# End of attention: the order of VectorE's and ScalarE's side work around the last norms, and the residual in the context's buffer

## The chip, the cores and the metric

One core of one Trainium2 chip runs the whole program. The time is device microseconds of one execution, from launch to end; of several executions the median is given. A profile is one execution recorded by the hardware profiler; its span runs from the first to the last instruction of the program. Five engines work side by side, each through its own instructions strictly in the order in which they stand in the built program: TensorE (PE; its weight loads are PEld), VectorE (DVE), ScalarE (ACT), GpSimd (POOL) and SyncE (SP), which here only issues transfers (DMA).

## The reference

A pre-norm block in float32 on 2048 rows of 1024: attention across the 32 heads of one position (each position's heads attend to each other, not to other positions), then a gated feed-forward whose weights are first rounded to the 16 NF4 levels in blocks of 64.

```python
q = (h @ wq.T + bq).reshape(B, S, H, D)       # k, v alike; h = layernorm(x)
scores = einsum('bshd,bstd->bsht', q, k) / sqrt(D)
context = einsum('bsht,bstd->bshd', softmax(scores), v)
x = x + context.reshape(B, S, E)
# feed-forward on layernorm(x); dq = round to NF4 times the block's largest absolute value
h = silu(y @ dq(w1).T) * (y @ dq(w2).T)       # y = layernorm(x)
x = x + h @ dq(w3).T
```

## The kernel before

**Tiles and stages.** The 2048 rows are 16 tiles of 128 rows, numbered 0 to 15, and 8 pairs `p`. Three sweeps run over the pairs: the projection to q, then to k with scores and softmax, then to v with the context product. The feed-forward follows, on blocks of 512 columns of a transposed, normalised x. The large products use seven products on quarter matrices in place of eight (`products` in attention, `Unit` in the feed-forward), so sums and differences of quarters are formed beforehand (`A`, `V`, the tiles `xU`) and the partial results are put together by copies on ScalarE and additions on VectorE.

**The side work.** While TensorE runs attention and the feed-forward, VectorE and ScalarE round the feed-forward's weights. The generator `background` does this in small steps: a step is one `sg` on ScalarE (L266, 128x1024) and one select-and-merge on VectorE that reads it (L267); there are also steps without ScalarE (L257, L259, L261), a block maximum with a reciprocal (L230, L237, L238), and scalings by the block's value (L218, 16 instructions of ScalarE, or L214, one of VectorE). The `sg` tile has two buffers, so the third step's ScalarE part waits for the first step's VectorE part. `advance(n)` puts the next n steps into the program. `flush` puts in the transposes of a finished weight (L178 on TensorE, copied by L179, combined by L185 to L194, stored by L197).

**What sets the order.** TensorE's instructions stand in the order in which the program writes them. On the other engines a scheduler orders them when the kernel is built, by when it thinks them ready. Two helpers bind it. `behind(kind)` sets a step's ScalarE part (kind "step") or scaling (kind "scale") behind the last copy that was passed to `marked`, if the kind is in `urgent["rule"]`. `turn()`, used by `advance`, sets the VectorE part of the steps behind the instruction in `held["behind"]`, if there is one.

**The end of the v sweep.** `gather(i, ...)` makes one tile's attention output, in two parts: the first half of the context product (L464, into PSUM), and then the second half with `residual`. That one transposes the result on VectorE out of PSUM into `cx` (L725, a single buffer), adds the row's x in place into `x1` (L729), sends the sum to `x1d` in memory in two halves (L731), and calls `normed(x1, x1)`: statistics (L133), their combination (L134), the inverse deviation on GpSimd (L137, L138), and the normalised tile written over x1 (L358). The context product has one PSUM tile of four banks, so the next tile's first half waits for this tile's L725. `part()` emits the next part in line, `keep_T(i)` transposes tile i's normalised x on TensorE (L768), copies it to `xT` (L769, marked), stores it (L774), and for each odd tile forms four differences `xU` on VectorE (L784, two buffers) and stores them (L785).

In the last pass of the v sweep (p = 7) the second half of tile 11, both halves of tile 12 and the first half of tile 13 are emitted. The five parts left, the second half of tile 13 and both halves of tiles 14 and 15, are put between the eight groups of matmuls of `plain_block`, which is the feed-forward's chunk 0 on the first 512 columns (L364 with `z<-xB,w0`; its gates are L895 and L896). Behind each part stands an `advance`. Then the first feed-forward unit starts: `first` makes z and copies it to g0 (L975), `middle` goes on accumulating into the same z bank, so each further product into z (L364 `z<-xT`) waits for the copy before it: g0 (L975), u2 (L982), u4 (L989).

SyncE's queue carries, in one order, the loads of x, weights and operands and the stores L731, L774, L785 and L197.

Of the kernel before, what the change touches and what calls it, by code (L numbers as in the profile page):

```python
# [14 lines left out]
ALU = mybir.AluOpType  # L15
# [16 lines left out]
TB = 512  # L32
# [37 lines left out]
def preln_block_kernel(  # L70
# [14 lines left out]
    nc = tc.nc  # L85
# [13 lines left out]
    x1d = [  # L99
        [tc.dram_tile([P, TB], FP, name=f"x1d{i}_{n}") for n in range(2)] for i in range(NT)  # L100
    ]
# [9 lines left out]
    hook = {"scale": "ACT"}  # L111

    urgent = {"last": None, "rule": ()}

    def marked(ins):

        urgent["last"] = ins.ins
# [6 lines left out]
    held = {"behind": None}  # L124

    def turn():

        return tc.issue_after(held["behind"]) if held["behind"] else nullcontext()

    def mean_var(pool, src, dst):  # L130
        st = pool.tile([P, 2, 6], FP, tag="st", name="st")
        for j in range(2):
            nc.vector.bn_stats(st[:, j, :], src[:, ts(j, 512)])  # L133
        nc.vector.bn_aggr(dst, st.rearrange("p a b -> p (a b)"))  # L134

    def inv_std(dst, var):
        nc.gpsimd.tensor_tensor(dst, var, eps, ALU.add)  # L137
        return nc.gpsimd.tensor_tensor(dst, dst, mhalf, ALU.pow)  # L138
# [141 lines left out]
    def advance(n):  # L280
        for _ in range(n):
            with turn():
                next(bg, None)

    def until(kind, c):
        while (kind, c) not in wd:
            if pending:
                flush(1)
            else:
                advance(1)  # L290
# [15 lines left out]
    NP = NT // 2  # L306
# [43 lines left out]
    def normed(src, dst, order=None):  # L350
        mv = small.tile([P, 2], FP, tag="mv", name="mv")
        rs = small.tile([P, 1], FP, tag="rs", name="rs")
        mean_var(small, src, mv)
        with tc.issue_after(order["last"]) if order else nullcontext():
            order_end = inv_std(rs, mv[:, 1:2])
        if order is not None:
            order["last"] = order_end.ins
        done = nc.vector.tensor_scalar(dst, src, mv[:, 0:1], rs, ALU.subtract, ALU.mult)  # L358
        hook["normed"] = done.ins
        return dst  # L360

    def mm4(dst, w, xop, start, stop):
        for k in range(4):
# [7 lines left out]
            )  # L371

    def products(A, fill, used=lambda name: None, apart=None):


# [216 lines left out]
    def load_A(src, p):  # L592
        t = pair.tile([P, 7, 4, P], FP, tag="A", name="A", bufs=2)
        nc.sync.dma_start(t, src[p])
        return t
# [81 lines left out]
    def part():  # L677
        if parts:
            next(parts[0])
            left_over[0] -= 1  # L680
            if left_over[0] == 0:
                parts.pop(0)
                left_over[0] = 2
# [38 lines left out]
    def residual(i, at, x1):  # L722

        cx = work.tile([P, E], FP, tag="cx", name="cx")
        nc.vector.transpose(  # L725
            cx.rearrange("p (h d) -> p d h", d=D),
            at[:, :, 0:256].rearrange("p c (s d) -> p d s c", d=D),
        )
        nc.vector.tensor_tensor(x1, x1, cx, ALU.add)  # L729
        for n in range(2):  # L730
            nc.sync.dma_start(x1d[i][n], x1[:, ts(n, TB)])  # L731
        return normed(x1, x1)

    ops = {}

# [51 lines left out]
    for p in range(NP):  # L787
        if p + 1 < NP:
            nextA = load_A(opV, p + 1)
        else:  # L790

            until("2", 0)
            nextA = work.tile([P, 4, 4, P], FP, tag="w0", name="w0")
            nc.sync.dma_start(nextA, wd["2", 0][:, 0:4])
        i = 2 * p - 4

        def fill(n):
            if n in (7, 2, 5, 4) and (p, n) != (1, 7):
                part()
            advance({7: 2, 6: 2, 5: 1, 3: 2}.get(n, 0))  # L800
            if n in (7, 4):
                flush(1)
            if n == 5 and i in x1n:
                keep_T(i, x1n.pop(i))
            if n == 3:
                if p == 0:
                    part()
                elif i + 1 in x1n:
                    keep_T(i + 1, x1n.pop(i + 1))

        cs = products(A, fill, (lambda name: None) if p + 1 < NP else next_op)
        flush(1)
        if p == 0:
            sweep.close()
            sweep = ExitStack()
            work = sweep.enter_context(
                tc.tile_pool(name="workv", bufs=1, side="right", reuse_waits="tile")
            )
        pl = load_tiles(pD, p, "pl", 3)
        for j in range(2):  # L820
            t = work.tile([P, 32, D], FP, tag="vd", name="vd", bufs=3)
            v_T(t, cs[j], vb_sb)
            parts.append(gather(2 * p + j, pl[j], t))
        advance(2)
        A = nextA
    hook["scale"] = "both"
    urgent["rule"] = ()
    left.close()


# [50 lines left out]
    def plain_block(w, tbp):  # L881

        hs = []
        for j in range(2):
            zs = []
            for m in range(2):
                z = ps_z.tile([P, TB], FP, tag="z", name="z")
                mm4(z, w[:, 2 * m], op(f"B1{j + 1}", tbp), True, False)
                yield
                mm4(z, w[:, 2 * m + 1], op(f"B2{j + 1}", tbp), False, True)  # L890
                zs.append(z)
                if not (j and m):
                    yield
            h = h0p.tile([P, TB], FP, tag=f"h{j}", name="h")
            nc.scalar.activation(h, zs[0], AF.Silu)  # L895
            nc.vector.tensor_tensor(h, h, zs[1], ALU.mult)  # L896
            hs.append(h)
        yield hs
# [6 lines left out]

    plain = plain_block(A, 0)
    i = NT - 4
    next(plain)  # L910
    next(plain)
    part()
    advance(1)
    next(plain)
    keep_T(i, x1n.pop(i))
    part()
    advance(2)
    flush()
    next(plain)
    part()  # L920
    advance(2)
    next(plain)
    keep_T(i + 1, x1n.pop(i + 1))
    part()
    advance(3)
    next(plain)
    part()
    advance(3)
    next(plain)
    keep_T(i + 2, x1n.pop(i + 2))  # L930
    hs = {0: next(plain)}
    advance(3)
    held["behind"] = hook["normed"]
    keep_T(i + 3, x1n.pop(i + 3))
    sweep.close()
    sweep_at.close()
# [20 lines left out]
    class Unit:  # L957
# [13 lines left out]
        def first(self):  # L971
            self.z = ps_z.tile([P, TB], FP, tag="z", name="z")
            self.mul(1, self.z, True, False)
            self.g0 = hp.tile([P, TB], FP, tag="g0", name="g0", bufs=2)
            nc.scalar.copy(self.g0, self.z)  # L975

        def middle(self):
            q = self.q = ps_q.tile([P, TB], FP, tag="q", name="q")
            self.mul(7, q, True, False)
            self.mul(6, self.z, False, False)  # L980
            u2 = self.u2 = hp.tile([P, TB], FP, tag="u2", name="u2")
            nc.scalar.copy(u2, self.z)  # L982
            r = ps_r.tile([P, TB], FP, tag="r", name="rr")
            self.mul(2, r, True, True)
            nc.vector.tensor_tensor(self.g0, self.g0, r, ALU.add)  # L985
            nc.scalar.activation(self.g0, self.g0, AF.Silu)
            self.mul(5, self.z, False, False)
            u4 = hp.tile([P, TB], FP, tag="u4", name="u4")
            nc.scalar.copy(u4, self.z)  # L989
            self.h = [new_h(), new_h()]  # L990
            nc.vector.tensor_tensor(self.h[1], u4, q, ALU.add)

# [195 lines left out]
    for n, (g, tbp) in enumerate(passes):  # L1188
        half, sides = None, []
        while now is not None and now.tbp == tbp and now.c in g:  # L1190
            unit = now
            unit.middle()
            if unit.c == min(g[-1], NFULL - 1):
                for c in [c for c in w3T if c not in g]:
                    del w3T[c]
                ask_w3(g)
            if g[-1] == NFULL and unit.c == NFULL - 1:
                half = Half(tbp)
                half.part(0)
                hs[unit.c] = unit.last()  # L1200
                half.part(1)
                hs[NFULL] = half.h
                now = None
            if units:
                now = Unit(*units.pop(0))
                now.first()
            if unit.c < PAIRED and unit.c % 2:
                side = Sides(hs[unit.c - 1], n == 0, len(sides))
                hs[unit.c] = unit.last(side.second)
                sides.append(side.both(hs[unit.c][0]))  # L1210
            elif half is None:
                hs[unit.c] = unit.last()
        if sides:
            down7(g, tbp, sides)
        else:
            down(g, tbp, hs)
        hs = {}
# [40 lines left out]
```

## Time and profile before

| | us |
|---|---|
| median of 4 runs | 2464.74 (2462.41 to 2465.62) |
| the profiled execution, its own time | 2467.89 |
| its span | 2466.1 |

Mean granted TensorE clock 0.991 of full speed.

| stretch, us | stage | PE busy | DVE busy | ACT busy |
|---|---|---|---|---|
| 535 to 745 | v sweep | 204.80 | 194.75 | 100.08 |
| 745 to 770 | its last pass | 22.92 | 20.54 | 13.96 |
| 770 to 835 | plain block, last norms, start of the first unit | 47.81 | 56.71 | 32.47 |
| 905 to 1000 | feed-forward, first group | 91.68 | 88.00 | 75.11 |
| 2200 to 2345 | feed-forward, side work done | 145.00 | 19.13 | 30.27 |
| 2345 to 2466 | last group | 112.52 | 30.20 | 7.16 |

The profile counts a matmul of float32 as two passes, so a group of four 128x512 matmuls is shown as eight. In the lines of a timeline the columns are: start, duration, engine, line of the code, operation, written and read tiles, shapes, count of merged instructions, and in brackets the idle time of the engine ahead of it and what ended it. Names of tiles are shortened to the variable's stem: `x` is x1, `r` the weight being rounded, `g` g0.

### The profile page before, as it was taken

What the parts mean: (1) busy time and instruction counts of PE and PEld (TensorE: products, weight loads), DVE (VectorE), ACT (ScalarE), POOL (GpSimd) and SP (SyncE); (2) the same over time, 40 slices, a digit from 0 to 9 for tenths busy, and PEclk for the clock granted to TensorE, in tenths of its full rate; (3) what the DMA queues carried; (4) which work ended last, traced back from release to release, by engine and by line L of the source; (5) the groups of instructions that cost most, each with busy time, mean ns of one, the idle gap of its engine ahead of it and who ended that gap; (6) DMA issues with size and microseconds to landing.
All of it is one profiled execution on the core that took longest, in us unless ns stands there. A gap on an engine that the chain in (4) does not pass through costs nothing.

```text
span 2466.1 us, 36345 instructions
## 1 busy us (share of the span) xinstructions
PE 2384.6 (97%) x14000; PEld 1115.5 (45%) x14000; DVE 2016.2 (82%) x2239; ACT 1511.9 (61%) x2819; POOL 289.3 (12%) x364
## 2 busy tenths in 40 slices
PE   8899999999998899999999999999999999999998
PEld 4444455545554344444444444444444444444433
DVE  8999888679899799898989989899898998861022
ACT  4556644134445578778787786977878778751200
POOL 1010000000000003030030301203012030020300
PEclk9999999999999999999999999999999999999999
DMA  8788643656779578485784858848588385772983
GB/s 320 274 299 340 244 154 123 227 210 218 237 236 320 192 268 171 141 172 186 280 185 141 175 167 297 176 149 181 161 295 193 126 187 162 276 168 76 179 307 123
DMA packets 179549, 513.87 MB, mean 208 GB/s; under 512 B 15984, under 2 KB 70256, under 8 KB 156976
## 3 DMA queue, kind: packets, MB, share of 16 engines
q1 hardware_dynamic: 138672, 438.08, 49.2%
q0 software_dynamic: 40704, 73.47, 18.4%
q8 instruction: 110, 1.80, 0.3%
q14 instruction: 63, 0.52, 0.1%
HBM read 283.69 MB, written 227.80 MB: 207 GB/s over the span
## 4 chain that ended last, share of the span: by engine, by line
DVE 27%; issue 18%; PE 11%; ACT 8%; DMA 4%; POOL 1%; DVEq 0%; POOLq 0%; ACTq 0%; SPq 0%
DVE r L267 18%; PE z L364 4%; DMA x1d<-acc 2%; ACT sg L266 2%; ACT wn L218 2%; PE q L364 2%; ACT r L218 1%; PE z L1070 1%; DVE r L259 1%; DVE r L261 1%; PE po L1151 1%; DVE am L230 1%; ACT acc L1083 1%; PE rr L364 1%; DMA xdT<-xU 1%
## 5 line engine op out<-in xcount | busy, mean ns | idle before, releaser
L267 DVE SCALAR_TENSOR_TENSOR r<-sg,r 128x1024 f32<-128x1024 f32 x780 | 945.8, 1213 | 81.6 <-ACT sg L266 48.1
L266 ACT ACTIVATE sg<-wn 128x1024 f32<-128x1024 f32 x780 | 814.2, 1053 | 306.5 <-DVE r L267 280.8
L1085 POOL DMA_DIRECT2D x1d<-acc x280 | 243.6, 921 | 1279.0 <-ACT acc L1083 1243.1
L364 PE MATMUL z<-xB,w 128*128 128x512 f32 x720 | 325.6, 599 | 5.9 <-ACT u L989 4.3
L364 PE MATMUL z<-xT,w 128*128 128x512 f32 x656 | 298.5, 598 | 12.1 <-ACT g L975 8.0
L364 PE MATMUL q<-xT,w 128*128 128x512 f32 x656 | 291.3, 592 | 0.0
L1070 PE MATMUL z<-w,h 128*128 128x512 f32 x496 | 230.7, 593 | 2.5 <-ACT acc L1083 2.5
L364 PEld LDWEIGHTS z<-xB,w 128*128 128x128 f32 x720 | 134.3, 191 | 169.4 <-issue 151.2
L364 PEld LDWEIGHTS z<-xT,w 128*128 128x128 f32 x656 | 122.4, 191 | 164.9 <-issue 138.2
L218 ACT ACTIVATE wn<-wn,rc 128x64 f32<-128x64 f32 x736 | 188.2, 338 | 8.9 <-DVE rc L238 8.9
L364 PEld LDWEIGHTS q<-xT,w 128*128 128x128 f32 x656 | 123.2, 190 | 148.6 <-issue 145.7
L364 PE MATMUL z<-wT,A 128*128 128x512 f32 x384 | 176.6, 603 | 0.0
L364 PE MATMUL q<-wT,A 128*128 128x512 f32 x384 | 172.7, 592 | 0.0
L1070 PE MATMUL y<-w,h 128*128 128x512 f32 x320 | 152.0, 596 | 3.6 <-DVE h L1048 3.1
L364 PE MATMUL z<-wB,A 128*128 128x512 f32 x320 | 150.3, 614 | 1.7 <-ACT u L383 1.7
L364 PE MATMUL rr<-xB,w 128*128 128x512 f32 x328 | 147.5, 592 | 0.0
L1070 PEld LDWEIGHTS z<-w,h 128*128 128x128 f32 x496 | 92.6, 190 | 116.2 <-issue 101.5
L218 ACT ACTIVATE r<-r,am 128x64 f32<-128x64 f32 x456 | 115.9, 341 | 14.6 <-DVE r L267 14.5
L1083 ACT COPY acc<-z 128x512 f32<-128x512 f32 x160 | 92.4, 584 | 36.6 <-PE z L1070 29.7
L364 PEld LDWEIGHTS q<-wT,A 128*128 128x128 f32 x384 | 72.1, 190 | 86.6 <-issue 83.9
L985 DVE TENSOR_TENSOR g<-g,rr 128x512 f32<-128x512 f32 x41 | 27.9, 681 | 100.4 <-PE rr L364 100.4
L137 POOL TENSOR_TENSOR rs<-mv,eps 128x1 f32<-128x1 f32 x32 | 18.0, 562 | 764.7 <-DVE mv L134 764.7
(136 smaller groups left out, 2734.7 us busy)
## 6 DMA issues: line engine op xcount, KB each, us to landing
x1d<-acc POOLq DMA_DIRECT2D x280, 256.0 KB, 6.4
wd<-wop SPq DMA_DIRECT2D x31, 2048.0 KB, 7.3
w<-wd SPq DMA_DIRECT2D x41, 1280.0 KB, 7.8
wn<-in_w_dram SPq DMA_DIRECT2D x63, 512.0 KB, 4.2
xT<-xdT SPq DMA_DIRECT2D x28, 1024.0 KB, 8.5
xB<-xdB SPq DMA_DIRECT2D x24, 1024.0 KB, 6.8
w<-wd SPq DMA_DIRECT2D x42, 512.0 KB, 4.3
w<-wd SPq DMA_DIRECT2D x10, 1536.0 KB, 7.7
```

Source lines behind the costliest of these rows:

```text
L218: nc.scalar.mul(dst[:, ts(n, BLOCK)], src[:, ts(n, BLOCK)], by[:, n : n + 1])
L230: nc.vector.tensor_reduce(am[:, :nb], v.rearrange("p (b e) -> p b e", e=BLOCK), AX.X, ALU.max, apply_absolute_value=True,)
L259: nc.vector.scalar_tensor_tensor(r, v, edge, r, ALU.is_lt, ALU.max)
L261: nc.vector.scalar_tensor_tensor(r, v, edge, r, ALU.is_gt, ALU.subtract)
L266: nc.scalar.activation(t, v, AF.Copy, bias=-edge * by, scale=by)
L267: nc.vector.scalar_tensor_tensor(r, t, code, r, ALU.min, ALU.max)
L364: nc.tensor.matmul(dst, w[:, k, :], xop[:, k, :], start=start and k == 0, stop=stop and k == 3, skip_group_check=True,)
L985: nc.vector.tensor_tensor(self.g0, self.g0, r, ALU.add)
L1070: nc.tensor.matmul(dst, side[n][:, ts(q, P)], w3T[g[2 * m]][:, W3[n]], start=start and m == 0, stop=stop and m == 1, skip_group_check=True,)
L1083: nc.scalar.copy(t, src)
L1085: nc.gpsimd.dma_start(x1d[8 * tbp + 2 * q + j][n], t, accum_op=ALU.add)
L1151: nc.tensor.matmul(po, hs[c][j][:, ts(q, P)], w3T[c][:, ts(n, 512)], start=(c == g[0]), stop=False, skip_group_check=True,)
```

## The change

- `residual` writes the sum of x and context into `cx` in place of `x1`; the stores to `x1d` read `cx`; `normed` reads `cx` and writes `x1`.
- The last pass of the v sweep emits 6 steps of side work in place of 9. In the plain block each of the five parts is followed by 3 steps (before: 1, 2, 2, 3, 3), and the block ends with 2 (before: 3). All in all 23 steps stand there, as before.
- `held["behind"]` is set to a tile's L358 after each of the five parts (before: once, after the last), so the VectorE parts of the steps written after a part stand behind the norm of that part's tile. A first half has no norm of its own; there it is the tile's before.
- `urgent["rule"]` stays ("scale", "step") until the first unit is written out (before: emptied at the end of the v sweep), and three copies of `Unit` are marked.

```diff
-        nc.vector.tensor_tensor(x1, x1, cx, ALU.add)
+        nc.vector.tensor_tensor(cx, x1, cx, ALU.add)
         for n in range(2):
-            nc.sync.dma_start(x1d[i][n], x1[:, ts(n, TB)])
-        return normed(x1, x1)
+            nc.sync.dma_start(x1d[i][n], cx[:, ts(n, TB)])
+        return normed(cx, x1)
...
-            advance({7: 2, 6: 2, 5: 1, 3: 2}.get(n, 0))
+            advance({7: 2, 6: 2, 5: 1, 3: 2 if p + 1 < NP else 0}.get(n, 0))
...
-        advance(2)
+        advance(2 if p + 1 < NP else 1)
         A = nextA
     hook["scale"] = "both"
-    urgent["rule"] = ()
...
+    def last_part(turns):
+        part()
+        held["behind"] = hook["normed"]
+        advance(turns)
+
...
-    part()
-    advance(1)
+    last_part(3)
     next(plain)
     keep_T(i, x1n.pop(i))
-    part()
-    advance(2)
+    last_part(3)
     flush()
     next(plain)
-    part()
-    advance(2)
+    last_part(3)
...
-    part()
-    advance(3)
+    last_part(3)
     next(plain)
-    part()
-    advance(3)
+    last_part(3)
     next(plain)
     keep_T(i + 2, x1n.pop(i + 2))
     hs = {0: next(plain)}
-    advance(3)
-    held["behind"] = hook["normed"]
+    advance(2)
...
-            nc.scalar.copy(self.g0, self.z)
+            marked(nc.scalar.copy(self.g0, self.z))
...
-            nc.scalar.copy(u2, self.z)
+            marked(nc.scalar.copy(u2, self.z))
...
-            nc.scalar.copy(u4, self.z)
+            marked(nc.scalar.copy(u4, self.z))
...
                 hs[unit.c] = unit.last()
+            urgent["rule"] = ()
```

## Prediction

> **What bounds the kernel now.** I read the page's busy times first, then the busy times by stretch, then the timelines of TensorE, VectorE and ScalarE in the stretch that the change touches.
>
> ```profile
> PE 2384.6 (97%) x14000; PEld 1115.5 (45%) x14000; DVE 2016.2 (82%) x2239; ACT 1511.9 (61%) x2819; POOL 289.3 (12%) x364
> core 0: us, PE busy (x) PEld busy (x) DVE busy (x) ACT busy (x) POOL busy (x), PEclk, DMA share, GB/s
> 755.00:835.00 80.00, 62.81 (x920) 33.31 (x918) 70.81 (x79) 41.31 (x75) 5.45 (x8) 0.88 0.81 265
> 835.00:905.00 70.00, 69.81 (x179) 31.57 (x178) 58.43 (x67) 54.04 (x112) 0.00 (x0) 0.99 0.58 218
> 1000.00:2200.00 1200.00, 1181.59 (x2992) 529.98 (x2991) 1095.97 (x1184) 950.55 (x1718) 195.05 (x224) 1.00 0.70 193
> ```
>
> TensorE is busy 97% of the span, so time can come only from its gaps. Between 755 and 835 it is busy 62.81 of 80 us, at a granted clock of 0.88; afterwards it hardly stops. Where it stops there:
>
> ```profile
> 784.90 1.54 PE L464 MATMUL cx<-vd,pl 32*32 32x32 f32 x128 [4.95 <-DVE cx L725]
> 786.37 4.90 PE L364 MATMUL z<-xB,w 128*128 128x512 f32 x8
> 801.11 0.26 PE L464 MATMUL cx<-vd,pl 32*32 32x32 f32 x8 [2.36 <-issue]
> 801.30 5.40 PE L364 MATMUL z<-xB,w 128*128 128x512 f32 x8
> 817.22 1.06 PE L768 MATMUL pt<-ident,x 128*128 128x128 f32 x8 [1.37 <-DVE x L358]
> 818.12 3.60 PE L364 MATMUL z<-xB,w 128*128 128x512 f32 x8
> 833.13 5.41 PE L364 MATMUL z<-xT,w 128*128 128x512 f32 x8 [7.97 <-ACT g L975]
> ```
>
> With 0.53 us at 797.52 the waits are 4.95 + 0.53 + 2.36 + 1.37 + 7.97 = 17.2 us. There is a second price: a group that takes 3.60 takes 4.90, 5.40 and 5.41 behind the longer waits (1.30 + 1.80 + 1.81 = 4.9 us). So at most 22.1 us can be had here. The two orders that cause it:
>
> ```profile
> 755.87 0.81 DVE L358 TENSOR_SCALAR x<-x,mv,rs 128x1024 f32<-128x1024 f32 x1 [4.39 <-DMA x1d<-x]
> 757.20 1.95 DVE L725 STREAM_TRANSPOSE cx<-cx 128x1024 f32<-128x1024 f32 x1
> 779.48 0.69 DVE L784 TENSOR_TENSOR xU<-xT,xU 128x512 f32<-128x512 f32 x1 [0.75 <-DMA xdT<-xU]
> 782.96 1.89 DVE L725 STREAM_TRANSPOSE cx<-cx 128x1024 f32<-128x1024 f32 x1
> 795.51 1.96 DVE L725 STREAM_TRANSPOSE cx<-cx 128x1024 f32<-128x1024 f32 x1
> 807.96 1.98 DVE L725 STREAM_TRANSPOSE cx<-cx 128x1024 f32<-128x1024 f32 x1 [0.63 <-PE cx L464]
> 816.26 0.81 DVE L358 TENSOR_SCALAR x<-x,mv,rs 128x1024 f32<-128x1024 f32 x1 [2.09 <-DMA x1d<-x]
> ```
>
> ```profile
> 827.73 3.93 ACT L218 ACTIVATE wn<-wn,rc 128x64 f32<-128x64 f32 x16 [0.37 <-DVE rc L238]
> 831.57 1.04 ACT L266 ACTIVATE sg<-wn 128x1024 f32<-128x1024 f32 x1
> 832.52 0.56 ACT L975 COPY g<-z 128x512 f32<-128x512 f32 x1
> ```
>
> The four L725 are tiles 12 to 15. TensorE's matmuls for z end at 821.6, but their copy stands on ScalarE behind six steps and 16 scalings and comes at 832.52.
>
> **The change part by part.** TensorE's and GpSimd's orders come out of the build unchanged; those of VectorE, ScalarE and SyncE differ from the v sweep on. I walk through the new orders with the durations above: transposition to addition 2.0, to statistics 1.2, to their combination 1.3, through GpSimd to L358 1.25 with VectorE idle (813.97 to 815.2), in all 5.8 us; a step of VectorE 1.13 from start to start, a half-width operation 0.6.
>
> *Residual in cx.* L358 no longer waits for the stores, but the next L725 does, since cx has one buffer. Tile 11's stores land at 755.74; tile 12's L725 then starts at about 755.8 in place of 757.2. Elsewhere in the sweep the stores land 2.0 to 4.6 us after issue and the next L725 comes 7 us or more after the issue: no cost, no gain. The 32 stores are the same in size and number.
>
> *Tile 13, gain 2.8.* No side step stands now between tile 12's norm and tile 13's L725, only the v tiles and the four L784. The fourth L784 still waits for a store (779.46); the DMA engines are 0.96 busy at 760 to 780, so I leave its landing where it is. L725 follows at 780.1; before, three more operations (L259, L185, L261) came between. TensorE waits until 782.1 for tile 14's first half, not 784.90: lead 2.8 us, its clock still low afterwards (2.1 us idle; the row with 2.08 us at 753.88 was followed by a group of 4.75).
>
> *Tile 14, minus 1.4.* L358 at 785.9; then five steps (5.7), L896 (0.6) and L259 (1.1) stand ahead of L725, which starts at 794.1 against 795.51. Before, four were spread inside the chain. TensorE arrives with 2.8 us lead, waits, and has 1.4 left. The 2.36 us of "issue" stays.
>
> *Tile 15, minus 1.5 and 1.8.* L725 stands behind two more differences, L261, L230 and four steps. The third step's ScalarE part stands behind L895, which waits for z (805.3), and the fourth L784 waits for a store issued at 805.8 that lands 3.9 to 4.7 us later, as at 802.60 and 807.35. So L725 starts at 810.6, later than 807.96. Its own chain is shorter (5.8 against 8.3 us): L358 at 816.4 against 816.26. TensorE's lead is gone, its wait is 2.9 in place of 1.37 us, and the group behind it pays the slow clock, 5.40 against 3.60. Lead -1.9.
>
> [...]
>
> *g0, plus 9.8.* On ScalarE three steps stand between the last L769 and L975, and the third starts once VectorE has consumed the one two before, at 821.8. The copy ends at 824.0, while TensorE is in the next product until 826.9. The 7.97 us and the 1.81 of slow clock are gone.
>
> *u4, minus 0.8.* Marked copies let the later steps queue behind them, but eight scalings, L986 (silu) and more scalings of the first unit still stand ahead of u4's copy, and L986 waits for L985, which stands behind VectorE's steps and the last two differences. These wait for tile 15's stores, issued at about 822.5. At 819.84 such a store took 4.1 us, behind an operand load of 1 MB (issued 815.37, landed 821.72); that load goes out near 811 now, so I take the 2.5 us of the row at 825.17. VectorE is then at L985 at 837.2, and L986, 8 scalings (1.95), one step (1.06) and L179 (0.5) put the end of u4's copy at 842.6. TensorE asks for it at 841.8. With 4.1 us it is 844.0, a wait of 2.2.
>
> Sum of lead at the third product into z, which began at 849.55 before: 2.8 - 1.4 - 1.5 - 1.8 + 9.8 - 0.8 = 7.1 us. Bounds of this walk: with u4's wait 2.2 and 1.5 us of slow clock behind it, 4.2; with u4 not late, 7.9.
>
> *What is owed.* By L985 VectorE has done 19 merging steps (L267) since tile 12's transposition, before it was 24: 5 x 1.13 = 5.7 us pushed into the feed-forward. The cover is VectorE's idle time, 70 - 58.43 = 11.6 us between 835 and 905. If it can't be used, TensorE pays, and 1.4 us of the lead are left. From 1000 to 2200 VectorE has 104 us idle in all, TensorE 18.4, so a debt is not carried on. The other orders in the feed-forward are reshuffled for some groups; of the 18.4 us spread in waits of under 1.6 us I expect no net change, plus or minus 3.
>
> *Moved transfers.* The second unit's big weight load (L850, 1280 KB) goes behind tile 13's stores in SyncE's queue; the unit needs it after 850, some 55 us later. Free.
>
> The profiled span 2466.1 becomes 2459.0. That execution took 2467.89, 3.15 above the median 2464.74; the same difference on the median gives 2464.74 - 7.1 = 2457.6.
>
> **The rivals.**
>
> *The waits vanish altogether.* If the stores land early and the steps before tiles 14 and 15 aren't late, 2.1 + 1.9 + 2.9 + 1.8 + 0.8 more go: 7.1 + 9.5 = 16.6, so 2448.1. For it: VectorE's work up to tile 15's L358 is five operations shorter. Against: two of the waits hang on DMA at 0.81 share.
>
> *The debt falls on TensorE.* 7.1 - 5.7 = 1.4: 2463.3. For it: TensorE's copies stand in ScalarE's queue among steps that wait for VectorE. Against: the 11.6 us.
>
> *The debt recurs: slower.* Place: ScalarE's queue in the first five units. If a step ahead of u2 and u4 waits each time for a late VectorE, TensorE loses 2.2 us at each: 5 x 2 x 2.2 = 22, against the lead before u4 of 7.9: 14.1 us slower, 2478.8. From six such waits on (13.2 - 7.9 = 5.3 us) it is measurably slower. It decides if VectorE is busy without a break from 835 to 1000. Against: the waits on u2 and u4 before are 4.0 and 4.3 us, 15 times, over the whole feed-forward.
>
> *It doesn't do what it says.* The steps held behind the norms only move in front of the next tile's L725, so the norms come no earlier; that is in the sum already. It can't come to nothing while L975 stands behind three steps in place of six and 16 scalings.
>
> **How the numbers follow.** Forecast 0.50, waits vanish 0.18, debt on TensorE 0.16, debt recurs 0.16. A change of 0.2%, 4.9 us, is about what can be told from none: below 2459.8 is faster, above 2469.7 slower. The forecast's own range is 2464.74 - 7.9 - 3 to 2464.74 - 4.2 + 3, that is 2454 to 2464; its likeliest value lies 2.2 below the limit, and I count three quarters of it as faster: 0.50 x 0.75 + 0.18 = 0.56. Same: 0.125 + 0.16 = 0.28. Slower 0.16. The range that holds 8 in 10 reaches from the first rival, 2448, to 2469, some 6 us beyond the third; the last case and the far tail of the first lie outside.
>
> **What would show it.** The 7.97 us wait on g at L975 gone, and the copy within 3 us of its matmuls. Tile 13's L725 at about 780, tile 15's near 810. No wait of L358 on `x1d`, and a wait of L725 on it at tile 12. A wait of TensorE on u4 of 1 to 2 us in the first unit. VectorE over 58.43 busy in the next 70 us. Wrong I'd be if TensorE's waits in the feed-forward grow, or if tile 15's norm comes much before 816 or after 820.

## The result, and the profile after

The changed kernel is slower: 2471.22 us median of 30 runs (2467.43 to 2476.43), the kernel before 2466.22 us median of 48 runs beside it (2458.59 to 2473.12). The ratio is 1.0019, 95% interval 1.0014 to 1.0025. The forecast of 2457.6 and its range up to 2469 were both too low. The profiled execution took 2467.65 us, 3.6 less than the median of its runs; its span is 2465.9 us, against 2466.1 before. One profile each therefore hides a loss of 5 us that the medians show, and a second profile of the changed kernel (span 2467.7) is used beside the first.

The page's busy times and the busy times by stretch, of the changed kernel (the columns are those shown for the kernel before):

```profile
PE 2384.5 (97%) x14000; PEld 1116.0 (45%) x14000; DVE 2017.4 (82%) x2239; ACT 1510.6 (61%) x2819; POOL 286.6 (12%) x364
```

```profile
core 0: us, PE busy (x) PEld busy (x) DVE busy (x) ACT busy (x) POOL busy (x), PEclk, DMA share, GB/s
755.00:835.00 80.00, 70.80 (x1074) 38.60 (x1073) 67.55 (x75) 38.01 (x71) 5.12 (x10) 0.96 0.83 274
835.00:905.00 70.00, 67.08 (x169) 30.26 (x168) 64.52 (x72) 56.30 (x116) 0.00 (x0) 0.98 0.63 237
1000.00:2200.00 1200.00, 1179.97 (x2988) 529.24 (x2987) 1099.27 (x1186) 954.03 (x1723) 195.25 (x224) 1.00 0.70 193
```

At the end of attention TensorE is busy 70.80 of 80 us where it was 62.81: 8.0 us more. The next 70 us give 2.7 back. TensorE's timeline there, of the changed kernel:

```profile
759.51 0.52 PE L464 MATMUL cx<-vd,pl 32*32 32x32 f32 x36 [1.73 <-issue]
761.57 4.61 PE L364 MATMUL z<-wB,A 128*128 128x512 f32 x8
...
786.65 1.26 PE L464 MATMUL cx<-vd,pl 32*32 32x32 f32 x109 [1.11 <-issue]
...
801.47 0.26 PE L464 MATMUL cx<-vd,pl 32*32 32x32 f32 x7 [1.81 <-issue]
801.66 3.70 PE L364 MATMUL z<-xB,w 128*128 128x512 f32 x8
...
818.23 1.94 PE L768 MATMUL pt<-ident,x 128*128 128x128 f32 x8 [3.71 <-DVE x L358]
819.96 4.42 PE L364 MATMUL z<-xB,w 128*128 128x512 f32 x8
...
845.55 5.36 PE L364 MATMUL z<-xB,w 128*128 128x512 f32 x8 [2.92 <-ACT u L987]
```

The wait of 7.97 us on g0 is gone, and so is the one of 4.95 us before tile 14's first half (a pause of 1.11 us without a releaser, "issue", stands inside that half). In their place stand 3.71 us for tile 15's norm (1.37 before) and 2.92 us for u4's copy (none before), each with a slow group behind it (4.42 and 5.36 us, against 3.70 at 801.66). VectorE's and ScalarE's lines that answer to those shown of before:

```profile
760.32 1.95 DVE L725 STREAM_TRANSPOSE cx<-cx 128x1024 f32<-128x1024 f32 x1 [1.47 <-DMA x1d<-cx]
...
781.33 1.92 DVE L725 STREAM_TRANSPOSE cx<-cx 128x1024 f32<-128x1024 f32 x1
...
795.85 1.90 DVE L725 STREAM_TRANSPOSE cx<-cx 128x1024 f32<-128x1024 f32 x1
...
811.54 1.98 DVE L725 STREAM_TRANSPOSE cx<-cx 128x1024 f32<-128x1024 f32 x1
...
817.27 0.81 DVE L358 TENSOR_SCALAR x<-cx,mv,rs 128x1024 f32<-128x1024 f32 x1 [0.93 <-POOL rs L138]
```

```profile
824.42 0.59 ACT L973 COPY g<-z 128x512 f32<-128x512 f32 x1 [0.33 <-PE z L364]
...
841.07 0.63 ACT L984 ACTIVATE g<-g 128x512 f32<-128x512 f32 x1 [2.33 <-DVE g L983]
841.60 2.00 ACT L218 ACTIVATE wn<-wn,rc 128x64 f32<-128x64 f32 x8
...
844.92 0.58 ACT L987 COPY u<-z 128x512 f32<-128x512 f32 x1
```

The copy of g0 starts as its matmuls end (819.96 + 4.42 = 824.38), where it came eleven us after them. The end of attention did much of what it was to do, so the loss must lie elsewhere. TensorE's order is the same in both kernels, so the same matmul can be found in both profiles, and its start after less its start before is the lag of the changed kernel. At 540 us of the profile before it is -1.3 us, at 734 us, ahead of the last norms, it is +5.7: the changed kernel loses 7 us in the v sweep, where the forecast had put nothing.

What happens there can be seen on VectorE. The same tile's norm and what follows, first in the kernel before, then in the changed one:

```profile
727.74 0.21 DVE L134 BATCH_NORM_AGGREGATE mv<-st 128x2 f32<-128x12 f32 x1
727.87 1.95 DVE L439 STREAM_TRANSPOSE vd<-ce 128x1024 f32<-128x1024 f32 x1
729.71 1.18 DVE L267 SCALAR_TENSOR_TENSOR r<-sg,r 128x1024 f32<-128x1024 f32 x1
730.80 0.80 DVE L358 TENSOR_SCALAR x<-x,mv,rs 128x1024 f32<-128x1024 f32 x1
```

```profile
731.47 0.21 DVE L134 BATCH_NORM_AGGREGATE mv<-st 128x2 f32<-128x12 f32 x1
732.61 0.81 DVE L358 TENSOR_SCALAR x<-cx,mv,rs 128x1024 f32<-128x1024 f32 x1 [0.93 <-POOL rs L138]
733.34 1.97 DVE L439 STREAM_TRANSPOSE vd<-ce 128x1024 f32<-128x1024 f32 x1
```

Before, L358 overwrote x1 and so had to wait for the stores that read it; the scheduler put L439 and a step into that time, and GpSimd worked out `rs` meanwhile. With the sum in `cx`, L358 has no store to wait for and stands straight behind L134. VectorE now stands still while GpSimd works out `rs`, and L439 and what follows it come behind that. One of the following is the addition L415, for which TensorE waits next: it starts 7.70 us after L134 (731.47 to 739.17), where it was 5.52 (727.74 to 733.26) and nothing waited for it. TensorE's timeline, of the changed kernel:

```profile
739.91 3.70 PE L364 MATMUL q<-wT,A 128*128 128x512 f32 x8 [1.34 <-DVE co L415]
```

The view of waits, VectorE, 600 to 745 us (total, times, longest), before and after:

```profile
DVE x L358 <- POOL rs L138: 1.2, 2, 0.7
```

```profile
DVE x L358 <- POOL rs L138: 6.3, 8, 0.9
```

### The profile page after: what moved, and what is told of

The parts are those of the page before. It is cut to its first block, busy times and chain, and to the rows that moved or that the text cites. A ratio compares the mean times of both kernels' runs of the same rounds, so it can differ in the third digit from the quotient of the medians.

```text
span 2465.9 us, 36334 instructions
## 1 busy us (share of the span) xinstructions
PE 2384.5 (97%) x14000; PEld 1116.0 (45%) x14000; DVE 2017.4 (82%) x2239; ACT 1510.6 (61%) x2819; POOL 286.6 (12%) x364
## 4 chain that ended last, share of the span: by engine, by line
DVE 28%; issue 18%; PE 11%; ACT 8%; DMA 4%; POOL 1%; DVEq 0%; POOLq 0%; SPq 0%; ACTq 0%
DVE r L267 18%; PE z L364 4%; ACT sg L266 2%; DMA x1d<-acc 2%; ACT wn L218 2%; PE q L364 2%; PE z L1068 1%; ACT r L218 1%; PE po L1149 1%; DVE r L259 1%; DVE r L261 1%; DVE am L230 1%; ACT acc L1081 1%; PE rr L364 1%; PE y L1068 1%
## 5 line engine op out<-in xcount | busy, mean ns | idle before, releaser
L218 ACT ACTIVATE wn<-wn,rc 128x64 f32<-128x64 f32 x736 | 188.3, 338 | 6.5 <-DVE rc L238 6.5
L218 ACT ACTIVATE r<-r,am 128x64 f32<-128x64 f32 x456 | 115.4, 340 | 19.6 <-DVE r L267 19.5
L364 PEld LDWEIGHTS z<-wT,A 128*128 128x128 f32 x384 | 70.9, 191 | 79.4 <-issue 76.5
```

The costliest lines, as they stand in the source:

```text
L218: nc.scalar.mul(dst[:, ts(n, BLOCK)], src[:, ts(n, BLOCK)], by[:, n : n + 1])
L364: nc.tensor.matmul(dst, w[:, k, :], xop[:, k, :], start=start and k == 0, stop=stop and k == 3, skip_group_check=True,)
```

## The experiments

Theory A was that the residual in `cx` loses the time in the v sweep, and that the end of attention gains; theory B that the feed-forward loses it. Each run was timed beside the kernel before on the same chip, and the ratios are to its runs there (medians 2465.9 to 2466.7 us); in brackets stands the 95% interval.

**The changed kernel again.**

> The changed kernel once more, against the kernel before on the same chip. Theory A (the loss is made in the v sweep by the residual in the context's buffer, the end of attention gains) and theory B (the loss is made in the feed-forward by the order of side work) both expect about 1.002 of the time before (+5 us). They differ in the profile: by A the matmuls of the v sweep fall behind those of the kernel before by some 10 us between 627 and 734, and the lag after the first unit's u4 (850) is about 8 us less than at 734; by B the lag at 734 changes from profile to profile and the lag grows after 900.

Measured: 2471.42 us, ratio 1.0014 (1.0005 to 1.0023). The second profile loses 6.7 us from 540 to 734, the first lost 7.0. From 734 to 853 it gains 8.6 (8.0), as A expects.

**The two halves of the change, each alone, and the buffer for the last tiles only.** The first takes the `cx` lines of the diff and nothing else, the second everything else; the third is the whole change with

```diff
-        nc.vector.tensor_tensor(cx, x1, cx, ALU.add)
+        sm = cx if i >= NT - 4 else x1
+        nc.vector.tensor_tensor(sm, x1, cx, ALU.add)
```

> The residual in the context's buffer alone; the orders of the end of attention are those of the kernel before. Theory A: slower by 6 to 10 us (1.0025 to 1.004); TensorE's lag behind the kernel before grows by some 10 us between 627 and 734 and VectorE waits for GpSimd's rs at L358 about 0.9 us a tile, 8 times or so between 600 and 745, in place of twice. Theory B: 0.999 to 1.001, no lag made in the v sweep.

> The orders of the end of attention alone (turns, what is held behind the norms, the marked copies, the rule to the end of the first unit); the residual stays in x1. Theory A: faster by 4 to 8 us (0.9968 to 0.9984), with no lag up to 740 and a lead of 5 to 8 us after 850 that lasts to the end. Theory B: slower by about 5 us (1.002), the lead at 850 being given back in the feed-forward.

> The whole change, but with the residual in the context's buffer for tiles 12 to 15 only. Theory A: faster than the kernel before by 4 to 8 us (0.9968 to 0.9984), since the v sweep up to tile 11 is as before. Theory B: slower by about 5 us (1.002).

Measured: `cx` alone 2474.05 us, 1.0025 (1.0016 to 1.0034), a lag of 12.2 us made between 540 and 734, the eight waits for `rs` of 6.3 us in all: A. VectorE's waits for stores of `xU` between 600 and 745 are 10.0 us there, 7.4 before, so `rs` isn't all that it waits longer for. The order alone 2465.52 us, 0.9994 (0.9985 to 1.0002): its sign speaks against B, but the gain of 4 to 8 us that A expected isn't there. The buffer for tiles 12 to 15 only 2463.41 us, 0.9987 (0.9979 to 0.9996): faster than before, but by 3.3 us, again less than A's 4 to 8. So A has the place of the loss right and the gain too large: in the profile of the order alone 6.1 us of lead at 838 are 1.8 at 853 and 0.8 at 2200.

**Is it the buffer or the place of L358?** In this kernel the sum stays in `cx` for all tiles, but L358 of tiles 0 to 11 is issued behind the addition or transposition that stood ahead of it before (a helper emits it late; the lines of this kernel are some 10 to 17 higher):

```diff
-        return normed(cx, x1)
+        return normed(cx, x1, defer=i < NT - 4)
...
+        finish_norm(first.ins)
...
+        finish_norm(turned.ins)
```

> The residual in the context's buffer alone, as in the run with that edit alone (1.0025), but for tiles 0 to 11 L358 is issued behind VectorE's next addition or transposition of the products, where it stood before. Theory A1 (the buffer frees L358 from its wait for the store, the scheduler then puts it straight behind L134, and VectorE stands 0.7 to 0.9 us a tile for GpSimd): lag behind the kernel before at most 2 us at 734, the 4 us gained at the end of attention stay: 0.998 to 0.9995. Theory A2 (the single buffer itself costs: L725 must wait for stores that read it, or the stores come later): still 1.002 to 1.003, lag at 734 above 8 us.

Measured: 2464.26 us, 0.9991 (0.9981 to 1.0001). Its timeline of VectorE has the old order back, and no wait:

```profile
627.51 0.21 DVE L134 BATCH_NORM_AGGREGATE mv<-st 128x2 f32<-128x12 f32 x1
627.64 1.95 DVE L455 STREAM_TRANSPOSE vd<-ce 128x1024 f32<-128x1024 f32 x1
629.48 1.19 DVE L267 SCALAR_TENSOR_TENSOR r<-sg,r 128x1024 f32<-128x1024 f32 x1
630.58 0.69 DVE L801 TENSOR_TENSOR xU<-xT 128x512 f32<-128x512 f32 x1
631.18 0.82 DVE L368 TENSOR_SCALAR x<-cx,mv,rs 128x1024 f32<-128x1024 f32 x1
```

The lag at 734 is 0.5 us, 1.2 less than at 540. VectorE's waits between 600 and 745 are 5.4 us for `xU` and none for `rs`, against 10.0 and 6.3 with `cx` alone. So the buffer itself costs nothing that shows; the place that the scheduler gave L358 costs 1.0025 - 0.9991 = 0.34%, some 8 us. Theory A1 holds in time and lag, though from 734 to 853 this kernel gains 1.8 us, not 4.

**The order part taken apart.** First the marked copies and the longer rule alone, then the turns alone (6 steps in the last pass, 3 after each part, and what is held behind the norms):

```diff
-    hook["scale"] = "both"
-    urgent["rule"] = ()
+    hook["scale"] = "both"
...
-            nc.scalar.copy(self.g0, self.z)
+            marked(nc.scalar.copy(self.g0, self.z))
```

> Of the order part only the marked copies of the first unit and the rule kept to its end; the turns and what is held behind the norms as before, the residual in x1. Theory C (g0's copy is early: the 7.97 us wait and 1.8 us of slow clock go, u4's copy then costs 2 to 3 us and 1.8 us of slow clock): lead of 5 to 6 us after 850, 0.9975 to 0.9985 of the time. Rival D (the feed-forward takes the lead back, as VectorE has the same work left): 0.9995 to 1.0005, the lead gone by 1000.

> Of the order part only the turns (6 steps in the last pass, 3 after each part, what is held behind the norms); no marked copies, the rule emptied at the end of the v sweep, the residual in x1. Theory G (the turns cost by themselves: tile 15's norm is late, TensorE waits 5 us or more for its L358 and again on u4): 1.0005 to 1.0015. Rival H (the turns are free, as the whole order part at 0.9994 and the marks alone at 0.9987 can't be told apart): 0.9985 to 1.0002.

Measured: the marks alone 2462.71 us, 0.9987 (0.9978 to 0.9995), between the two expectations; the lead is 8.7 us at 853 and 5.2 at 1000, so C has the gain and D part of what follows. u4 is waited for 0.23 us only, against what C expected. The turns alone 2470.46 us, 1.0019 (1.0010 to 1.0028): theory G, and more than it said, though the wait on u4 that G expected isn't there. VectorE's and TensorE's timelines of the turns alone:

```profile
786.55 0.81 DVE L358 TENSOR_SCALAR x<-x,mv,rs 128x1024 f32<-128x1024 f32 x1 [5.39 <-DMA x1d<-x]
```

```profile
817.29 1.94 PE L768 MATMUL pt<-ident,x 128*128 128x128 f32 x8 [4.88 <-DVE x L358]
833.99 6.48 PE L364 MATMUL z<-xT,w 128*128 128x512 f32 x8 [6.18 <-ACT g L974]
```

With the sum still in x1, tile 13's L358 waits for the stores, and the steps that could fill that time are held behind it: VectorE stands for 5.39 us (5.35 in the profile of the order alone). So the turns want the residual in `cx` at the last four tiles; by this reading the buffer for these tiles made 0.9987 out of the order's 0.9994, but the two intervals overlap, so it rests on this wait and isn't shown by the times. Nor do the times show a gain from the turns: the marks alone are at 0.9987 too, and of the parts of the change only they are faster by themselves. And without the marks g0's copy is still late: 6.18 us of waiting.

**u4's copy.** ScalarE's lines of the changed kernel show what it stands behind: the silu of g0 (L984), which itself waits 2.33 us for VectorE, and 8 scalings. In the kernel with `cx` for the last tiles, the first unit's silu is set behind u4's copy:

```diff
+            if urgent["rule"]:
+                with tc.issue_after(urgent["last"]):
+                    nc.scalar.activation(self.g0, self.g0, AF.Silu)
```

> The kernel with the buffer for tiles 12 to 15 only (0.9987 of the time before) and, in the first unit, the silu of g0 set behind u4's copy on ScalarE, so that u4's copy doesn't stand behind an operation that waits for VectorE's L984. Theory C: the wait of 2.66 us on u4 and 1.8 us of slow clock go: 0.9965 to 0.9975. Rival D: lead given back in the feed-forward, 0.9983 to 0.999.

Measured: 2460.52 us, 0.9981 (0.9972 to 0.9990), between the two expectations; the interval overlaps that of the kernel it starts from (0.9979 to 0.9996), so the time alone proves no gain. The profile shows what changed: TensorE has no wait on u4 any more, and from 838 to 853 it loses nothing where it lost 4.6. ScalarE's timeline:

```profile
836.08 0.56 ACT L989 COPY u<-z 128x512 f32<-128x512 f32 x1
836.54 0.58 ACT L179 COPY wop<-ptw 128x512 f32<-128x512 f32 x1
837.02 0.63 ACT L992 ACTIVATE g<-g 128x512 f32<-128x512 f32 x1
```

**The other wait on a store.** In the changed kernel VectorE waits before tile 13's L725 for the stores of `xU`, which has two buffers:

```profile
776.74 0.69 DVE L784 TENSOR_TENSOR xU<-xT 128x512 f32<-128x512 f32 x1 [1.14 <-DMA xdT<-xU]
780.73 0.69 DVE L784 TENSOR_TENSOR xU<-xT,xU 128x512 f32<-128x512 f32 x1 [3.30 <-DMA xdT<-xU]
```

Three buffers (the bias of v is loaded later for it, into the place of that of q), first in the kernel with `cx` for the last tiles, then in the kernel before; a third kernel has the marks, `cx` for the last tiles and three buffers, with the old turns, and a fourth the new turns with u4's copy ahead of the silu as well:

```diff
-            u[n + 1] = work.tile([P, 4, P], FP, tag="xU", name="xU", bufs=2)
+            u[n + 1] = work.tile([P, 4, P], FP, tag="xU", name="xU", bufs=3)
```

> The kernel with the buffer for tiles 12 to 15 only (0.9987 of the time before), with three buffers of xU in place of two (the bias of v takes the place of that of q to make room). Theory E (tile 13's L725 is late since VectorE waits 4.99 us for a store of xU): that L725 comes 4 us earlier, TensorE's wait of 4.48 us for tile 14's first half is below 1 us, 0.9965 to 0.9978. Rival F (the stores themselves are the limit there: the next difference or tile 15's norm waits instead): 0.9982 to 0.999.

> The kernel before with three xU buffers alone. Theory E (waits for stores of xU on VectorE set the last norms' time; 0.9987 to 0.9966 on the other kernel): faster by 3 to 6 us, 0.9975 to 0.9988, though g0's wait of 8 us stays. Rival F: 0.9995 to 1.0005, since g0's copy stands behind the same steps, and these behind the same norm.

> The kernel before with the marked copies and the rule to the end of the first unit (0.9987 alone), the buffer for tiles 12 to 15 and three xU buffers; the turns as before. Theory G (the turns cost): below the kernel that has all these and the turns (0.9966): 0.9945 to 0.9960, without a wait on u4. Rival H: 0.9962 to 0.9972.

> The kernel with the buffer for tiles 12 to 15 only, with three xU buffers (0.9966) and the first unit's silu of g0 behind u4's copy. Theory C: the wait of 2.92 us on u4 and some 3 us of slow clock behind it go as well: 0.9940 to 0.9955. Rival D (given back in the feed-forward): 0.9962 to 0.9972.

Measured: 2458.05 us, 0.9966 (0.9954 to 0.9978); in the kernel before 2456.85 us, 0.9966 (0.9953 to 0.9978), more than E expected; marks with old turns 2457.11 us, 0.9957 (0.9944 to 0.9969); all together 2451.65 us, 0.9942 (0.9930 to 0.9954), in C's expectation. E's mechanism shows in VectorE's timeline of the first of the four: tile 13's L725 starts at 769.89, where the kernel with two buffers had 778.93, and what is left to wait for is TensorE. TensorE's own wait of 4.48 us for it is gone.

```profile
768.46 0.69 DVE L787 TENSOR_TENSOR xU<-xT,xU 128x512 f32<-128x512 f32 x1 [0.95 <-DMA xdT<-xU]
769.89 1.98 DVE L727 STREAM_TRANSPOSE cx<-cx 128x1024 f32<-128x1024 f32 x1 [0.74 <-PE cx L464]
```

In the kernel before with three buffers the gain doesn't lie where E put it. TensorE still waits for tile 13's L725, and longer (4.95 us before); what it saves is at g0's copy, which the scheduler now put ahead of the 16 scalings (6.1 us from 822 to 838), and some 3.7 us between 745 and 757, where the pause of 2.08 us at 753.88 and the group of 4.75 us behind it are gone. Why that pause goes isn't shown. TensorE's and ScalarE's timelines of this kernel:

```profile
779.30 1.54 PE L464 MATMUL cx<-vd,pl 32*32 32x32 f32 x128 [5.79 <-DVE cx L727]
823.86 3.70 PE L364 MATMUL z<-xT,w 128*128 128x512 f32 x8 [3.54 <-ACT g L977]
```

```profile
823.25 0.57 ACT L977 COPY g<-z 128x512 f32<-128x512 f32 x1
823.71 3.93 ACT L218 ACTIVATE wn<-wn,rc 128x64 f32<-128x64 f32 x16
```

The comparison of the old turns with the new under three buffers (0.9957 against 0.9966) is inconclusive: the first lies in G's range, but the intervals overlap. The last of the four is 14.4 us faster than the kernel before; its busy times at the end of attention (TensorE 71.66 of 80 us, 62.81 before):

```profile
755.00:835.00 80.00, 71.66 (x946) 36.85 (x945) 71.32 (x82) 41.77 (x76) 3.41 (x8) 0.98 0.77 252
```

**All profiles side by side.** Change of TensorE's lag behind the kernel before, us, by stretch of the profile before (+ is time lost; one profile each; "734 to 785" runs from tile 12's end to tile 14's first half, "785 to 822" to the end of tile 15's norm, "822 to 838" has g0's copy, "838 to 853" u4's):

| kernel | 540 to 734 | 734 to 785 | 785 to 822 | 822 to 838 | 838 to 853 | 853 to 2200 |
|---|---|---|---|---|---|---|
| changed | +7.0 | -5.4 | +2.3 | -9.9 | +5.1 | +2.0 |
| changed, second profile | +6.7 | -4.8 | +4.1 | -10.0 | +2.1 | +3.7 |
| `cx` alone | +12.2 | -3.0 | -2.1 | +0.7 | 0.0 | +1.6 |
| `cx`, L358 late | -1.2 | -1.5 | -0.8 | +0.5 | 0.0 | +1.3 |
| order alone | +0.1 | -4.2 | +7.9 | -9.9 | +4.3 | +1.1 |
| turns alone | +1.2 | -6.0 | +8.3 | -0.7 | 0.0 | -0.5 |
| marks alone | -1.9 | -3.8 | +4.8 | -9.9 | +0.5 | +3.3 |
| turns, marks, `cx` for tiles 12 to 15 | +1.8 | -3.1 | +4.7 | -9.9 | +4.6 | +1.2 |
| turns, marks, `cx` for tiles 12 to 15, u4 first | -1.2 | -5.1 | +5.4 | -10.0 | 0.0 | +2.3 |
| turns, marks, `cx` for tiles 12 to 15, three `xU` | -1.7 | -9.1 | +1.2 | -9.9 | +7.0 | +0.4 |
| three `xU` in the kernel before | -1.6 | -3.4 | +0.8 | -6.1 | 0.0 | -0.1 |
| marks, `cx` for tiles 12 to 15, three `xU` | -1.1 | -6.9 | +5.6 | -9.9 | 0.0 | +1.2 |
| turns, marks, `cx` for tiles 12 to 15, three `xU`, u4 first | -2.8 | -9.3 | +2.3 | -9.9 | +0.8 | +4.0 |

The first column tells how much profiles differ where the code is alike: the kernels with the old norm in the v sweep and two buffers lie between -1.9 and +1.8, those with L358 straight behind L134 between +6.7 and +12.2.

## Why the prediction was wrong, point by point

- **The step that failed** is "Elsewhere in the sweep the stores land 2.0 to 4.6 us after issue and the next L725 comes 7 us or more after the issue: no cost, no gain". It priced the wait that moves to L725, and that was right: L725 waits 1.47 us at tile 12, and no wait of it on a store shows on VectorE between 600 and 745. It didn't ask what stands behind the wait that was *removed*. L358's wait for the store had made the scheduler put VectorE's other work ahead of it, and that work hid GpSimd's 0.7 to 0.9 us. The runs put 0.34% on it, about 8 us (`cx` alone against `cx` with L358 late). No rival had this case either; all of them lay at the end of attention or behind it. Its signs of being wrong lay there too, where they couldn't show this loss. How the loss reaches TensorE, 7 to 12 us between 540 and 734, is not fully taken apart. All of VectorE's waits between 600 and 745 together (for `rs`, for stores of `xU` and for steps of ScalarE) are 9.1 us before, 14.8 in the changed kernel, 17.9 with `cx` alone and 7.3 with L358 late. TensorE's granted clock adds to the loss: from 540 to 734 it is at 0.50 for 6.83 us in the changed kernel (from 630.47, behind a wait of 2.14 us for L218; the group at 633.63 takes 5.42 us), and for 3.41 us before (from 621.57).
- **Tile 13** was right in time, and its size is not shown: L725 at 781.33 and, with `cx` for the last tiles, 778.93 (forecast 780.1). From 734 to 785 the changed kernel gains 5.4 us with the sweep's delay in it, the other 3.1 (forecast 2.8). But 2.6 of these 3.1 are made by 767, ahead of the wait, where a pause of 2.08 us, before with a group of 4.75 us behind it, is 1.27; the wait itself is 4.48 in place of 4.95. That 3.1 is near 2.8 is luck. TensorE's timeline of the kernel with `cx` for the last tiles:

```profile
752.12 0.52 PE L464 MATMUL cx<-vd,pl 32*32 32x32 f32 x37 [1.27 <-issue]
780.88 1.53 PE L464 MATMUL cx<-vd,pl 32*32 32x32 f32 x128 [4.48 <-DVE cx L725]
```

- **Tiles 14 and 15** were right in time and in sum. L725 at 795.85 and 811.54 (794.1 and 810.6), L358 at 817.27 (816.4), the wait 3.71 us (2.9). The three terms 1.4 + 1.5 + 1.8 = 4.7 are what the kernel with `cx` for the last tiles lost from 785 to 822; the changed kernel, which comes 5 us late to the last pass, lost 2.3 and 4.1 in its two profiles. The parts of the 4.7 differ from the forecast's: 1.0 up to 800, 1.7 won back where the pause of 2.36 us is 1.47 and the group behind it takes 3.70 us in place of 5.40, 5.4 at tile 15's norm. And the marks alone, with the old turns, lose 4.8 there as well (a wait of 4.47 us for tile 15's L358), so that the turns cause this loss, as the forecast had it, isn't shown.
- **g0** was right: +9.8 forecast, 9.9 to 10.0 measured in every kernel that has the marks, and 0.7 with the turns alone.
- **u4 was mis-sized**: 0.8 us, with bounds of 2.2 for the wait and 1.5 for the clock. Measured 5.1 and 2.1 in the two profiles, 4.6 with `cx` for the last tiles. The copy came where it was to come in that kernel (842.45 to 843.03, forecast end 842.6), but TensorE asked for it at 840.4, not 841.8, and the group behind the wait of 2.66 us was slow by 1.8 us. The forecast used the wait at its likely value and left the clock to the bound; in the changed kernel's two profiles waits on u4 of 2.92 and 1.80 us have groups of 5.36 and 3.70 us behind them.
- **The sum** of the walk, 7.1 us, is near the 8.0 and 8.6 that the changed kernel gained from 734 to 853, but partly by chance: a TensorE that comes late waits less, as `cx` alone shows (3.0 and 2.1 gained with the old order). Without that delay the same walk is worth 3.1 - 4.7 + 9.9 - 4.6 = 3.7 us (3.3 by the medians). The forecast differs from it by 3.4, of which u4 makes 3.8. By the medians, from the forecast's -7.1 to the measured +5.0 are 12.1 us: 8.3 that go with `cx` at the first twelve tiles, and 3.8 that are left at the end of attention and behind it.
- **What is owed** was about right: VectorE is busy 64.52 us from 835 to 905 in place of 58.43, within the cover. From 853 on 2.0 and 3.7 us are given back, where 3 were allowed. The third rival, by which the waits on u2 and u4 grow in each of the first units, fails: behind the first unit's they come to 8.4 us in all, 8.3 before.
- In sum for the first profile: 7.0 - 5.4 + 2.3 - 9.9 + 5.1 + 2.0 = +1.1 us from 540 to 2200, where the forecast had -7.1; with the -1.3 at 540 that is the -0.2 by which the two spans differ. The medians say +5.0; the profiled execution lies 3.6 under its median, that of before 1.7 above the 2466.22 of its runs.
- **The second half of the change carries a cost that the walk didn't split off**: the turns are worth 4.4 us of loss alone. The forecast's sum didn't need this, but a walk of each part without the other would have had to price the 5.39 us.

## What to carry to other kernels

Where an edit takes away a wait, look at what the scheduler had put in front of the waiting instruction: that work was hiding other latencies too, here GpSimd's 0.7 to 0.9 us, and it moves behind. Restrict such an edit to the places where the wait ended last (four tiles of sixteen here), or pin the instruction where it stood. Before reordering work around a wait on a store, try a further buffer for what is stored: a third one of 2 KB a partition gave 0.34%, the whole order part alone nothing that could be measured. Then look where the gain lies: here much of it came from an order that the scheduler changed, not from the wait that the buffer was to shorten.

## What the hardware showed

How long TensorE idles doesn't by itself decide whether the group behind is slow. In the changed kernel 1.73 us of idling at 759.51 is followed by a group of 4.61 us, 1.81 us at 801.47 by one of 3.70, both shown above. In its second profile the wait on u4 is 1.80 us and the group behind it takes 3.70 us; in the first it is 2.92 us, and the group takes 5.36 us. TensorE's timeline in the second profile:

```profile
848.99 3.70 PE L364 MATMUL z<-xB,w 128*128 128x512 f32 x8 [1.80 <-ACT u L987]
```

The forecast put the slow clock behind waits of 2.1 and 2.9 us, by rows of the kernel before: groups of 4.75 and 5.40 us behind pauses of 2.08 and 2.36 us, one of 3.60 us behind 1.37. Taken with the rows above, they show no limit on the length of a pause.

The granted clock that the traces record tells more. Between 216 and 2460 us the profile before has it at half, 0.50, from 508.93, 621.57, 754.69, 781.99, 802.47, 829.78 and 2437.46 on, each time for 3.41 us, from 781.99 and 829.78 for 6.83. The changed kernel's first profile has it so from 507.59, 630.47, 760.18, 818.21, 845.51 and 2436.13 on, each time for 3.41 us, from 630.47 for 6.83. In each of the two profiles these starts lie whole multiples of one length apart (75.09 us from 754.69 to 829.78 are 22 times 3.413, 85.33 us from 760.18 to 845.51 are 25 times 3.413). These are busy times in stretches of that length, with the columns as above: first the changed kernel around its wait of 2.92 us on u4, then the kernel before with three `xU` around its wait of 3.54 us on g0 (823.86, shown above):

```profile
842.10:845.52 3.42, 0.53 (x2) 0.00 (x0) 1.63 (x2) 3.42 (x11) 0.00 (x0) 1.00 0.00 0
845.52:848.93 3.41, 3.38 (x4) 1.50 (x5) 3.41 (x6) 2.35 (x3) 0.00 (x0) 0.50 0.02 5
```

```profile
818.71:822.12 3.41, 1.61 (x4) 0.38 (x2) 3.03 (x5) 2.11 (x2) 0.00 (x0) 1.00 0.83 220
822.12:825.54 3.42, 1.68 (x4) 0.87 (x5) 3.28 (x5) 3.26 (x10) 0.00 (x0) 1.00 1.04 357
825.54:828.95 3.41, 3.41 (x9) 1.52 (x8) 1.78 (x2) 3.41 (x11) 0.00 (x0) 1.00 0.41 173
```

The shorter wait lies almost whole in one stretch (2.89 us idle), and the next stretch is at half clock, 0.50. The longer one falls on two (1.80 and 1.74 us), and the clock stays at 1.00. From 860 to 2200 us neither the profile before nor the changed kernel's first has the clock below 1.00; the most that TensorE idled there in one stretch, counted on from those at half clock, is 1.52 us (969.73) and 1.75 us (968.39). The half clock at 2437.46 and 2436.13 follows on stretches with 2.18 and 2.76 us of idling. Ahead of 860 us less was enough: in the changed kernel half clock follows on 1.72 us in the stretch from 756.77 and on 1.52 us in that from 504.18, while 1.64 us in that from 261.83 is followed by a clock of 1.00. So no limit on the idling in one stretch can be drawn from the two profiles either.
